# Two small PSUM tiles share the outcome's bank, and the routing work changes its steps: linear attention and mixture of experts on one core

## The chip, the cores and the metric

The kernel runs on one core of a Trainium2 chip. The metric is the device time of the whole program in microseconds (us). Five engines work from their own instruction queues and wait for one another by semaphores: TensorE (PE) multiplies matrices and writes to PSUM; VectorE (DVE) and ScalarE (ACT) read PSUM and SBUF; GpSimd (POOL) reads SBUF and issues the indirect DMAs; SyncE (SP) issues the plain DMAs. All data is fp32.

## The reference, cut to what matters

x has 4 batches of 2048 tokens with 256 features. Two sublayers are added to it, each scaled by rows that come from a small conditioning vector (`sa, ca, ga, sb, cb, gb`).

```python
h = _layernorm(x) * (1 + ca) + sa
q, k, v = (phi(h @ Wq), phi(h @ Wk), h @ Wv)     # phi = elu + 1, 16 heads of 16
S = S + k_t[:, None] * v_t[None, :]; z = z + k_t # running over the tokens
num = S . q_t ; den = max(z . q_t, 1e-6)
x = x + ga * ((num / den) @ w_out.T)
h = _layernorm(x) * (1 + cb) + sb
logits = h @ w_router.T                          # 8 experts, the two best per token
keep = position_in_expert < capacity             # a running count over the tokens, 1280 each
y = sum_e combine[:, e] * (silu(h @ w_gate.T) @ w_down[e].T)
x = x + gb * y
```

## The kernel before

The 8192 tokens are cut into 16 **groups** of 512 (`G`), each of 4 tiles of 128. The main loop runs over s = 0 to 64, `g, j = divmod(s, 4)`: one **step** j per tile. The order of the instructions of PE, ACT, DVE and POOL is the order of the program text (`manual_schedule`), so the loop's body is a hand-written pipeline over several groups. While the attention of group g runs, the keys, queries, values and denominators of `nxt` = g+1 are made, group `nrm` = g+2 is normalised and its keys projected, group `far` = g+3 gets its sums, group `prv` = g-1 is normalised for the second sublayer and its router logits and ranks are found, and group `old` = g-2 gets its positions and slots and is sent off, row by row, to a list per expert in DRAM. Group 14 takes a branch of its own (`early`), and group 15 is the `tail`. After the loop comes the expert phase: the lists are read back in blocks, multiplied with the gate and down matrices, and added to the output by indirect DMAs.

What each step does, with the names that matter below:

- At its head every step has the scores of its tile (L494, into the four banks of `psc`), masked by VectorE (L500) to `at`; `attend` (L570) for the tile of the step before; `keep_state` (L514); and `take_out`, in which ScalarE copies the outcome and the state's gain from the bank `po` to `both` (L525) and POOL adds the state up (`s_acc` L538, `s_msk` L540). `from_state` (L557) ends the step with the first products for the next `po`. `done()` is the output projection of the tile before (`pw` L588), its addition to x (L589) and its statistics (L325); each step calls it once.
- Step 0: two query projections (`pq` L375), `second_moments` and `deviations` (mean and spread for both norms; ScalarE's squares L309, POOL's L295, L296, L313, L315, L317), first half of `running_keys` (a scan on VectorE, L433, and POOL's product with q, L438).
- Step 1: `keys_by_token`, `positions(old)`, second half of `running_keys`, `values` (L397, copied by L405), `normalise` of `nrm`, `shift_rows(old)` (adds the row `sb`, L618).
- Step 2: `denominators` (`pd` L446, then `den` L451 and `rden` L453 on VectorE), `second_norm(prv)`, `to_features` of `nrm` (`pta`), `scaled_q` (`pr` L464 from `rden`, written to the banks of `psc`; L471 reads it), `dispatch(old)` (the slots: fourteen small VectorE instructions, L731 to L753), `to_features` of `prv` (`ptm`).
- Step 3: `logits(prv)` (`pl` L640, copied to `lgT`), `scale_rows(prv)` (POOL L612), `send(old, 0, 3)`, `heads_apart` (`qeo` L484), the first k projection of `nrm`, `logits_by_token` (`lt` L653), `ranks` (L669 to L699: VectorE finds maximum and difference, ScalarE the exponential L672, VectorE the rest, POOL the counts), `done()`, the second k projection, `finish_keys` (L389), `sums(far)` (ScalarE L282).

PSUM has 8 banks. `psc` takes four, `po` one, and every other product takes one of three that go round (`bank()`). A tile in such a bank keeps it until its last reader is done:

```python
ps = ctx.enter_context(tc.tile_pool(name="ps", bufs=3, space=PSUM))
...
ps_sc = tokens.enter_context(tc.tile_pool(name="ps_sc", bufs=1, space=PSUM))
ps_o = tokens.enter_context(tc.tile_pool(name="ps_o", bufs=1, space=PSUM))
...
def bank(name):
    return ps.tile([P, 512], F32, tag="bank", name=name)
```

Of the kernel before, what the change touches and what calls it, by code (L numbers as in the profile page):

```python
# [36 lines left out]
F32 = mybir.dt.float32  # L37
AF = mybir.ActivationFunctionType
ALU = mybir.AluOpType
AX = mybir.AxisListType  # L40

P = 128
# [14 lines left out]
GATE_EPS = 1e-6  # L57
I32 = mybir.dt.int32
SLOTS = NE * CAP
O_GB, O_CW, O_TOK, W = D, 2 * D, 2 * D + NE, 2 * D + NE + 4  # L60
FAR = 65536.0
HB = 3
# [5 lines left out]
def adaln_block(ctx: ExitStack, tc, x, wqkvT, woutT, wrT, wgT, wdT, cT, wmod, out):  # L68
# [8 lines left out]
    def bank(name):  # L77
        return ps.tile([P, 512], F32, tag="bank", name=name)
# [207 lines left out]
    def second_moments(g):  # L286
# [8 lines left out]
        nc.gpsimd.tensor_scalar(ve[:, :NT], mv[:, :, 1], LN_EPS, None, ALU.add)  # L295
        nc.gpsimd.tensor_scalar(nm[:, :NT], mv[:, :, 0], -1.0, None, ALU.mult)  # L296

    def deviations(m, a):

        nm = G_.pop("nm")  # L300
        ve = G_.pop("ve", None)
        lo, hi = 0 if m is not None else NT, 2 * NT if a is not None else NT
        if ve is None:
            ve = small.tile([P, 2 * NT], F32, tag="ve", name=f"vea_{a}")
        if a is not None:
            xn = G_["xna", a]
            sq = small.tile([P, NT], F32, tag="sqa", name=f"sqa_{a}")
            for j in range(NT):
                nc.scalar.activation(  # L309
                    xn[:, j, :], xs[a][:, j, :], AF.Square, bias=nm[:, NT + j : NT + j + 1],  # L310
                    accum_out=sq[:, j : j + 1],
                )
            nc.gpsimd.tensor_scalar(ve[:, NT:], sq, 1.0 / D, LN_EPS, ALU.mult, ALU.add)  # L313
        rstd = small.tile([P, 2 * NT], F32, tag="rstd", name=f"rstd_{m}_{a}")
        nc.gpsimd.tensor_tensor(rstd[:, lo:hi], ve[:, lo:hi], mhalf[:, lo:hi], ALU.pow)  # L315
        nmr = small.tile([P, 2 * NT], F32, tag="nmr", name=f"nmr_{m}_{a}")
        nc.gpsimd.tensor_tensor(nmr[:, lo:hi], nm[:, lo:hi], rstd[:, lo:hi], ALU.mult)  # L317
        G_["ns", "m"] = nmr[:, :NT], rstd[:, :NT]
        G_["ns", "a"] = nmr[:, NT:], rstd[:, NT:]
# [117 lines left out]
            )  # L437
            nc.gpsimd.tensor_tensor(G_["qs", g][:, h, :], zc[:, h, :], G_["q", g][:, h, :], ALU.mult)  # L438

    def denominators(g):  # L440

        zq = G_["qs", g]
        pd = bank(f"pd_{g}")
        for h in range(NH):
            for j in range(NT):
                nc.tensor.matmul(  # L446
                    pd[32 * j : 32 * j + 32, :P], hpick[:, h, :], zq[:, h, j * P : (j + 1) * P],
                    start=(h == 0), stop=(h == NH - 1),
                )
        den = small.tile([P, P], F32, tag="den", name=f"den_{g}")  # L450
        nc.vector.tensor_scalar(den, pd[:, :P], DEN_EPS, None, ALU.max)  # L451
        rden = small.tile([P, P], F32, tag="rden", name=f"rden_{g}")
        inst = nc.vector.reciprocal(rden, den)  # L453
        G_["rden", g] = rden
        return inst
# [191 lines left out]

    state = {}

    def logits_by_token(part):  # L650
        g, j0, n = part
        lt = G_["lt", part] = bank(f"lt_{g}_{j0}")
        nc.tensor.transpose(lt[:, : 32 * n], G_.pop(("lgT", part))[: 32 * n, :], ident[: 32 * n, : 32 * n])  # L653

    def ranks(part, count=nc.gpsimd):
        g, j0, n = part
        if ("lt", part) not in G_:
            logits_by_token(part)
        lt = G_.pop(("lt", part))
        lg = lt[:, : 32 * n].rearrange("p (j e) -> p j e", j=n)[:, :, :NE]  # L660

        def tile_(name, shape, **kw):
            return small.tile([P, NT] + shape, F32, tag=name, name=f"{name}_{g}_{j0}", **kw)[:, :n]

        def wide(t):
            return t.unsqueeze(2).to_broadcast([P, n, NE])

        mx = tile_("mx", [])
        nc.vector.tensor_reduce(mx, lg, AX.X, ALU.max)  # L669
        gt_ = tile_("gates", [NE])  # L670
        nc.vector.tensor_tensor(gt_, lg, wide(mx), ALU.subtract)  # L671
        nc.scalar.activation(gt_, gt_, AF.Exp)  # L672
        sm = tile_("sm", [])
        nc.vector.tensor_reduce(sm, gt_, AX.X, ALU.add)
        nc.vector.reciprocal(sm, sm)
        nc.vector.tensor_tensor(gt_, gt_, wide(sm), ALU.mult)

        shape = [P, n, NE, NE]
        other = gt_.unsqueeze(2).to_broadcast(shape)
        own = gt_.unsqueeze(3).to_broadcast(shape)  # L680
        ahead = tile_("ahead", [NE, NE], bufs=1)
        nc.vector.tensor_tensor(ahead, other, own, ALU.is_gt)
        tie = tile_("tie", [NE, NE], bufs=1)
        nc.vector.tensor_tensor(tie, other, own, ALU.is_equal)
        nc.vector.tensor_tensor(tie, tie, tri8.unsqueeze(1).to_broadcast(shape), ALU.mult)
        nc.vector.tensor_tensor(ahead, ahead, tie, ALU.add)
        mask = tile_("mask", [NE])
        rank = tile_("rank", [NE])
        nc.vector.tensor_reduce(rank, ahead, AX.X, ALU.add)
        nc.vector.tensor_scalar(mask, rank, 1.5, None, ALU.is_lt)  # L690


        cnt = small.tile([P, NT + 1, NE], F32, tag="cnt", name=f"cnt_{g}_{j0}")
        if "cnt" not in state:
            count.memset(cnt[:, 0, :], 0.0)
        else:
            count.tensor_copy(cnt[:, 0, :], state["cnt"])
        for j in range(n):
            count.tensor_tensor(cnt[:, j + 1, :], cnt[:, j, :], mask[:, j, :], ALU.add)  # L699
        state["cnt"] = cnt[:, n, :]  # L700
        G_["route", part] = gt_, mask, rank, cnt
# [157 lines left out]
    with tc.manual_schedule(engines={ET.PE, ET.Activation, ET.DVE, ET.Pool}):  # L859
# [40 lines left out]
        for s in range(NG * NT + 1):  # L900
# [21 lines left out]
                logits(prv)  # L922
            if prv is not None and j == 3 and not early:
                scale_rows(prv)
            if last is not None:
                attend(*last)
            grow = g < NG and not (g % GPB == GPB - 1 and j == NT - 1)
# [4 lines left out]
            if tail:  # L932
# [27 lines left out]
                else:  # L960
# [15 lines left out]
                    positions(p15b)  # L976
                    dispatch(p15b)
                    send(p15b, 0, 4)
            if old is not None and j == 3 and not early:
                send(old, 0, 3)  # L980
            if s == 0:
                free_slots(2, project(1, "k", 0, D, 2))
                free_slots(3, project(1, "k", 1, D, 2))
# [8 lines left out]
            elif j == 0:  # L992
# [8 lines left out]
                    deviations(g - 1 if prv is not None else None, nrm)  # L1001
                if nxt is not None:
                    running_keys(nxt, (0,))
            elif j == 1:
                if nxt is not None:
                    keys_by_token(nxt)
# [5 lines left out]
                if nxt is not None:  # L1012
                    running_keys(nxt, (1,))
                if g >= 3:
                    send((g - 3, 0, NT), 3, 6)
                if nxt is not None:
                    values(nxt, 0)
                    values(nxt, 2)
                if nrm is not None:
                    normalise((nrm, 0, NT), "a", xs[nrm], G_["xna", nrm])  # L1020
                if old is not None:
                    shift_rows(old)
                if early:
                    to_features(prv, "m", 2)
                    dispatch(old)
                if g + 4 < NG:
                    load_x(g + 4)
            elif j == 2:
                if g >= 3:
                    send((g - 3, 0, NT), 6, 8)  # L1030
                if nxt is not None:
                    denominators(nxt)
                if early:
                    logits_by_token(prv)
                    scale_rows(prv)
                    send(old, 0, 4)
                elif prv is not None:
                    second_norm(prv)
                if nrm is not None:
                    to_features((nrm, 0, NT), "a", 0)  # L1040
                done()
                if nxt is not None:
                    scaled_q(nxt)
                if early:
                    ranks(prv)
                elif old is not None:
                    dispatch(old)
                if prv is not None and not early:
                    to_features(prv, "m", 2)
            else:  # L1050
                if nxt is not None:
                    heads_apart(nxt, (0,))
                if nrm is not None:
                    project(nrm, "k", 0, D, 2, later=True)
                if nxt is not None:
                    heads_apart(nxt, (1,))
                if prv is not None and not early:
                    logits_by_token(prv)
                    ranks(prv)
                done()  # L1060
                if early:
                    send(old, 4, 8)
                    positions(prv)
                    dispatch(prv)
                    shift_rows(prv)
                if nrm is not None:
                    project(nrm, "k", 1, D, 2, later=True)
                if nrm is not None:
                    finish_keys(nrm)
                if g % GPB == GPB - 1 and g + 1 < NG:  # L1070
                    gated_out(g // GPB + 1)
                if far is not None:
                    sums(far)
            last = None
            if g < NG:
                from_state(g, j)
# [64 lines left out]
```

## Time and profile before

| | |
|---|---|
| time, median of 3 runs | 910.64 us (909.93 to 918.53) |
| the profiled execution: time, span of its instructions | 915.75 us, 913.8 us |
| mean granted TensorE clock | 0.96 |
| busy: PE, DVE, POOL, ACT | 823.0, 568.2, 477.1, 419.0 us |
| main loop (scores of group 0 to the last sends) | about 62 to 600 us |
| expert phase | about 604 to 914 us |

In the profile, a row of a timeline gives the start, the duration, the engine, the line of the kernel, the operation, the tile written and the tiles read, and in brackets how long the engine had been idle and what ended that. A group of instructions is given as one row with count, busy time, mean, and idle time before it. "PEld" is the loading of weights on TensorE, which runs beside its multiplications. PEclk is the share of the full clock that TensorE was granted.

### The profile page before, as it was taken

The numbers are of one execution on the slowest core, as the hardware profiler recorded it, in microseconds if no ns is written. First come the engines' busy times: TensorE is split into PE (matmuls) and PEld (weight loads), VectorE is DVE, ScalarE is ACT, GpSimd is POOL, SyncE is SP. The second block draws the span as 40 slices with busy tenths as digits, with TensorE's granted clock in tenths as the row PEclk, the third lists the DMA queues.
The fourth block names the chain that finished last, engine by engine and source line by source line (L and its number), as shares of the span: only waits on it lengthen the run. The fifth ranks groups of instructions, "written<-read, shape, count | busy, mean of one in ns | idle before, by whom it ended". The sixth has DMA issues, their size and how long they took to land.

```text
span 913.8 us, 20612 instructions
## 1 busy us (share of the span) xinstructions
PE 823.0 (90%) x8245; PEld 576.5 (63%) x8245; DVE 568.2 (62%) x1158; ACT 419.0 (46%) x972; POOL 477.1 (52%) x605
## 2 busy tenths in 40 slices
PE   6899979999999899999999976539999999999995
PEld 4477657567567567567667555326776767767764
DVE  3667768988888888888988886513333333333331
ACT  4557656656567567566566423212222222222220
POOL 2323446575586586576676586523443444434434
PEclk9999989999999999999999989659999999999998
DMA  8499851331442242432121111255665656545233
GB/s 307 135 358 347 188 110 72 124 136 66 129 136 68 105 136 69 120 111 77 61 76 55 49 49 39 66 200 134 148 138 106 134 112 145 110 100 112 35 34 41
DMA packets 75111, 108.25 MB, mean 118 GB/s; under 512 B 9578, under 2 KB 47218, under 8 KB 75016
## 3 DMA queue, kind: packets, MB, share of 16 engines
q1 hardware_dynamic: 47672, 68.91, 24.8%
q0 software_dynamic: 21760, 31.99, 16.3%
q10 hardware_dynamic: 5584, 6.04, 2.0%
q8 instruction: 65, 1.06, 0.5%
q14 instruction: 30, 0.25, 0.1%
HBM read 45.07 MB, written 74.69 MB: 131 GB/s over the span
## 4 chain that ended last, share of the span: by engine, by line
PE 66%; DVE 15%; issue 6%; POOL 5%; ACT 4%; DMA 2%; POOLq 0%; DVEq 0%; ACTq 0%; SPq 0%
PE ph L821 14%; PE pe L834 13%; PE pq L375 6%; PE pv L397 5%; PE psc L494 5%; PE pk L375 5%; PE po L570 5%; PE pw L588 4%; DVE at L500 3%; PE po L557 3%; DVE sel L751 2%; DVE qs L471 2%; POOL slots L770 2%; PE pte L810 2%; POOL out_dram L843 1%
## 5 line engine op out<-in xcount | busy, mean ns | idle before, releaser
L843 POOL DMA_INDIRECT out_dram<-y,tok x80 | 123.3, 1542 | 180.7 <-DVE y L839 126.2
L500 DVE TENSOR_TENSOR at<-psc,tri 128x1024 f32<-128x1024 f32 x128 | 150.1, 1214 | 29.2 <-PE psc L494 28.8
L770 POOL DMA_INDIRECT slots<-hrow,idx x128 | 129.4, 1011 | 52.5 <-issue 36.4
L821 PE MATMUL ph<-hTe,wg_sb 128*128 128x512 f32 (+1 forms) x384 | 153.5, 527 | 0.0
L834 PE MATMUL pe<-wd,hid 128*128 128x256 f32 x640 | 150.5, 379 | 0.0
L827 DVE SCALAR_TENSOR_TENSOR hid<-th,ph 128x512 f32<-128x512 f32 (+1 forms) x96 | 57.5, 599 | 146.3 <-ACT th L826 146.3
L834 PEld LDWEIGHTS pe<-wd,hid 128*128 128x128 f32 x640 | 121.6, 190 | 37.0 <-issue 23.0
L826 ACT ACTIVATE th<-ph 128x512 f32<-128x512 f32 (+1 forms) x96 | 50.5, 526 | 156.4 <-PE ph L821 156.4
L821 PEld LDWEIGHTS ph<-hTe,wg_sb 128*128 128x128 f32 x384 | 70.4, 193 | 39.0 <-issue 32.5
L375 PE MATMUL pk<-hTa,wqkv_sb 128*128 128x512 f32 x128 | 69.3, 671 | 22.6 <-DVE gates L671 22.6
L494 PE MATMUL psc<-qeo,k 32*128 32x256 f32 x1024 | 74.7, 405 | 2.4 <-DVE qs L471 1.0
L588 PE MATMUL pw<-wob,both 128*128 128x256 f32 x236 | 63.2, 391 | 7.8 <-ACT both L525 5.5
L570 PE MATMUL po<-at,vpad 128*32 128x128 f32 x2048 | 69.8, 278 | 0.0
L839 DVE SCALAR_TENSOR_TENSOR y<-pe,rows 128x256 f32<-128x256 f32 x80 | 38.7, 484 | 49.6 <-PE pe L834 49.6
L570 PEld LDWEIGHTS po<-at,vpad 128*32 128x32 f32 x2048 | 53.9, 111 | 17.1 <-issue 16.9
L375 PE MATMUL pq<-hTa,wqkv_sb 128*128 128x512 f32 x128 | 61.3, 604 | 0.0
L494 PEld LDWEIGHTS psc<-qeo,k 32*128 32x128 f32 x1024 | 47.8, 188 | 19.7 <-issue 13.3
L397 PE MATMUL pv<-wqkv_sb,hTa 128*128 128x256 f32 x256 | 59.2, 384 | 0.0
L588 PEld LDWEIGHTS pw<-wob,both 128*128 128x128 f32 x236 | 41.9, 192 | 25.1 <-issue 10.1
L813 ACT COPY hTe<-pte 128x512 f32<-128x512 f32 (+1 forms) x48 | 24.7, 514 | 70.8 <-PE pte L810 70.6
L375 PEld LDWEIGHTS pk<-hTa,wqkv_sb 128*128 128x128 f32 x128 | 23.5, 201 | 46.7 <-issue 44.9
L397 PEld LDWEIGHTS pv<-wqkv_sb,hTa 128*128 128x128 f32 x256 | 47.6, 190 | 6.5 <-issue 0.4
(166 smaller groups left out, 1348.3 us busy)
## 6 DMA issues: line engine op xcount, KB each, us to landing
slots<-free SPq DMA_DIRECT2D x80, 262.0 KB, 5.1
rows<-slots SPq DMA_DIRECT2D x16, 1048.0 KB, 6.1
x<-in_x_dram SPq DMA_DIRECT2D x16, 512.0 KB, 6.1
out_dram<-x SPq DMA_DIRECT2D x16, 512.0 KB, 2.9
hrow<-mod_d SPq DMA_DIRECT2D x48, 128.0 KB, 3.5
rows<-slots SPq DMA_DIRECT2D x8, 524.0 KB, 7.6
wd<-in_wdT_dram ACTq DMA_DIRECT2D x8, 512.0 KB, 4.6
slots<-hrow,idx POOLq DMA_INDIRECT x128, 2.9
```

The costliest lines, as they stand in the source:

```text
L375: nc.tensor.matmul(pq, wqkv_sb[:, k, o + h * P : o + (h + 1) * P], hT[:, k, :], start=(k == 0), stop=(k == NH - 1))
L397: nc.tensor.matmul(pv[:, i * D : (i + 1) * D], hT[:, k, (j + i) * P : (j + i + 1) * P], wqkv_sb[:, k, 2 * D : 3 * D], start=(k == 0), stop ...
L494: nc.tensor.matmul(psc[:, a, h], kT[r : r + 32, h, cols], qeo[r : r + 32, h, :, cols], start=True, stop=True,)
L500: masked = nc.vector.tensor_tensor(at, psc[:, 2 * m : 2 * m + 2].rearrange("p i h q t -> p (i h q) t"), tri.unsqueeze(1).to_broadcast([P, ...
L570: nc.tensor.matmul(po[32 * a : 32 * a + 32, h * P : (h + 1) * P], vp[:, j, h * 4 + a, q : q + 2, :], att[a // 2][:, a % 2, h, q, :], start ...
L588: nc.tensor.matmul(pw[:, :D], oT[:, h, :], wob[:, h, :], start=(h == 0), stop=(h == NH - 1))
L770: row = nc.gpsimd.indirect_dma_start(out=slots[:, :], out_offset=bass.IndirectOffsetOnAxis(ap=idx[:, c, j : j + 1], axis=0), in_=hr[:, j0 ...
L821: nc.tensor.matmul(ph[:, :m], wg_sb[:, k, f * P : (f + 1) * P], hTs[b][:, k, :m], start=(k == 0), stop=(k == NH - 1),)
L826: nc.scalar.activation(th[:, :m], ph[:, :m], AF.Tanh, scale=0.5)
L827: nc.vector.scalar_tensor_tensor(hids[b][:, f, :m], th[:, :m], 1.0, ph[:, :m], ALU.add, ALU.mult)
L834: nc.tensor.matmul(pe[:, :D], hids[b][:, f, j * P : (j + 1) * P], wds[e][:, f, :], start=(f == 0), stop=(f == NF - 1),)
L843: put = nc.gpsimd.indirect_dma_start(out=out[:, :], out_offset=bass.IndirectOffsetOnAxis(ap=toks[b][:, j : j + 1], axis=0), in_=y, in_offs ...
```

## The change

Two small tiles leave the three banks that go round: `pd` (the denominators, 128 columns) and `lt` (the logits by token, 128 columns) are put into columns 320 to 447 of the bank of `po`, whose columns 0 to 319 hold the outcome and the state's gain. `denominators` follows `to_features` of `nrm` instead of leading it. `done()` is called in the middle of `ranks`, ahead of the exponential. ScalarE's passes that use no bank go to the heads of steps, ahead of `take_out`: `squares` (out of `deviations`) in step 0, `second_norm` in step 2, `sums` in step 3. `normalise` of `nrm` goes ahead of `values`. `shift_rows` moves from step 1 to step 0, `dispatch` from step 2 to step 1, and the eight sends of a group now lie in steps 2 (three), 3 (three) and the next step 1 (two).

```diff
+O_SMALL = D + NH * 32
...
+    def squares(a):
+
+        xn, nm = G_["xna", a], G_["nm"]
+        sq = G_["sq", a] = small.tile([P, NT], F32, tag="sqa", name=f"sqa_{a}")
+        for j in range(NT):
+            nc.scalar.activation(
+                xn[:, j, :], xs[a][:, j, :], AF.Square, bias=nm[:, NT + j : NT + j + 1],
+                accum_out=sq[:, j : j + 1],
+            )
+
     def deviations(m, a):
 
+        if a is not None and ("sq", a) not in G_:
+            squares(a)
...
-            for j in range(NT):
-                nc.scalar.activation(
-                    xn[:, j, :], xs[a][:, j, :], AF.Square, bias=nm[:, NT + j : NT + j + 1],
-                    accum_out=sq[:, j : j + 1],
-                )
...
-    def denominators(g):
+    def denominators(g, beside=False):
...
-        pd = bank(f"pd_{g}")
+        pd = G_["po"][:, O_SMALL : O_SMALL + P] if beside else bank(f"pd_{g}")[:, :P]
...
-    def logits_by_token(part):
+    def logits_by_token(part, beside=False):
         g, j0, n = part
-        lt = G_["lt", part] = bank(f"lt_{g}_{j0}")
+        lt = G_["po"][:, O_SMALL : O_SMALL + P] if beside else bank(f"lt_{g}_{j0}")
+        G_["lt", part] = lt
...
-    def ranks(part, count=nc.gpsimd):
+    def ranks(part, count=nc.gpsimd, meanwhile=None):
...
+        if meanwhile is not None:
+            meanwhile()
         nc.scalar.activation(gt_, gt_, AF.Exp)
...
                 scale_rows(prv)
+            if prv is not None and j == 2 and not early:
+                second_norm(prv)
+            if not tail and j == 0 and s > 0 and nrm is not None:
+                squares(nrm)
+            if not tail and j == 3 and far is not None:
+                sums(far)
             if last is not None:
                 attend(*last)
...
-            if old is not None and j == 3 and not early:
-                send(old, 0, 3)
+            if old is not None and j in (2, 3) and not early:
+                send(old, 3 * (j - 2), 3 * (j - 1))
...
                     running_keys(nxt, (0,))
+                if old is not None:
+                    shift_rows(old)
             elif j == 1:
...
                 if g >= 3:
-                    send((g - 3, 0, NT), 3, 6)
+                    send((g - 3, 0, NT), 6, 8)
+                if nrm is not None:
+                    normalise((nrm, 0, NT), "a", xs[nrm], G_["xna", nrm])
                 if nxt is not None:
                     values(nxt, 0)
                     values(nxt, 2)
-                if nrm is not None:
-                    normalise((nrm, 0, NT), "a", xs[nrm], G_["xna", nrm])
-                if old is not None:
-                    shift_rows(old)
                 if early:
                     to_features(prv, "m", 2)
+                if old is not None:
                     dispatch(old)
...
             elif j == 2:
-                if g >= 3:
-                    send((g - 3, 0, NT), 6, 8)
-                if nxt is not None:
-                    denominators(nxt)
                 if early:
...
-                elif prv is not None:
-                    second_norm(prv)
                 if nrm is not None:
                     to_features((nrm, 0, NT), "a", 0)
+                if nxt is not None:
+                    denominators(nxt, beside=True)
                 done()
                 if nxt is not None:
                     scaled_q(nxt)
                 if early:
                     ranks(prv)
-                elif old is not None:
-                    dispatch(old)
...
                 if prv is not None and not early:
-                    logits_by_token(prv)
-                    ranks(prv)
-                done()
+                    logits_by_token(prv, beside=True)
+                    ranks(prv, meanwhile=done)
+                else:
+                    done()
...
-                if far is not None:
-                    sums(far)
```

More of the change, by code (lines that the diff above doesn't have):

```diff
@@ L305, in deviations @@
         if a is not None:
-            xn = G_["xna", a]
-            sq = small.tile([P, NT], F32, tag="sqa", name=f"sqa_{a}")
-            for j in range(NT):
-                nc.scalar.activation(
-                    xn[:, j, :], xs[a][:, j, :], AF.Square, bias=nm[:, NT + j : NT + j + 1],
-                    accum_out=sq[:, j : j + 1],
-                )
-            nc.gpsimd.tensor_scalar(ve[:, NT:], sq, 1.0 / D, LN_EPS, ALU.mult, ALU.add)
+            nc.gpsimd.tensor_scalar(ve[:, NT:], G_.pop(("sq", a)), 1.0 / D, LN_EPS, ALU.mult, ALU.add)
         rstd = small.tile([P, 2 * NT], F32, tag="rstd", name=f"rstd_{m}_{a}")
@@ L446, in denominators @@
                 nc.tensor.matmul(
-                    pd[32 * j : 32 * j + 32, :P], hpick[:, h, :], zq[:, h, j * P : (j + 1) * P],
+                    pd[32 * j : 32 * j + 32, :], hpick[:, h, :], zq[:, h, j * P : (j + 1) * P],
                     start=(h == 0), stop=(h == NH - 1),
@@ L450, in denominators @@
         den = small.tile([P, P], F32, tag="den", name=f"den_{g}")
-        nc.vector.tensor_scalar(den, pd[:, :P], DEN_EPS, None, ALU.max)
+        nc.vector.tensor_scalar(den, pd, DEN_EPS, None, ALU.max)
         rden = small.tile([P, P], F32, tag="rden", name=f"rden_{g}")
```

## Prediction

> **What bounds the kernel now.** I read the page's engine sums first, then its costliest groups for a TensorE line with idle time, then the timeline engine by engine.
>
> ```profile
> PE 823.0 (90%) x8245; PEld 576.5 (63%) x8245; DVE 568.2 (62%) x1158; ACT 419.0 (46%) x972; POOL 477.1 (52%) x605
> L375 PE MATMUL pk<-hTa,wqkv_sb 128*128 128x512 f32 x128 | 69.3, 671 | 22.6 <-DVE gates L671 22.6
> ```
>
> PE is 90% busy, and its largest idle item that one line owns is 22.6 us before the key projection, ended by VectorE's L671. Asked for the readers of `lt`, the trace gives twelve such waits: one in the fourth step (j = 3) of each of groups 2 to 13. The timeline of PE in group 8, with the same place in group 7:
>
> ```profile
> 305.04 3.38 PE L375 MATMUL pk<-hTa,wqkv_sb 128*128 128x512 f32 x4 [2.20 <-DVE gates L671]
> ...
> 332.19 1.15 PE L494 MATMUL psc<-qeo,k 32*128 32x256 f32 x16
> ...
> 336.66 0.27 PE L653 MATMUL lt<-ident,lgT 128*128 128x128 f32 x1
> 336.77 1.03 PE L588 MATMUL pw<-wob,both 128*128 128x256 f32 x4
> 339.73 1.95 PE L375 MATMUL pk<-hTa,wqkv_sb 128*128 128x512 f32 x4 [1.93 <-DVE gates L671]
> ```
>
> The second k projection wants one of three banks, and `lt` sits in it until VectorE has read it. VectorE is late, as its timeline (and POOL's, last row) shows:
>
> ```profile
> 334.34 2.02 DVE L751 SCALAR_TENSOR_TENSOR sel<-rank,slot 128x32 f32<-128x32 f32 x1
> ...
> 336.92 2.34 DVE L500 TENSOR_TENSOR at<-psc,tri 128x1024 f32<-128x1024 f32 x2
> ...
> 339.39 0.19 DVE L671 TENSOR_TENSOR gates<-lt,mx 128x32 f32<-128x32 f32 x1
> ...
> 339.88 0.19 DVE L674 TENSOR_REDUCE sm<-gates 128x4 f32<-128x32 f32 x1 [0.29 <-ACT gates L672]
> ...
> 344.80 2.34 DVE L500 TENSOR_TENSOR at<-psc,tri 128x1024 f32<-128x1024 f32 x2
> ...
> 359.24 2.36 DVE L500 TENSOR_TENSOR at<-psc,tri 128x1024 f32<-128x1024 f32 x2 [1.38 <-PE psc L494]
> ...
> 361.83 0.95 DVE L453 RECIPROCAL rden<-den 128x128 f32<-128x128 f32 x1
> ```
>
> ```profile
> 333.94 2.37 POOL L612 TENSOR_TENSOR hrow<-hrow,modr 128x1024 f32<-128x1024 f32 x1
> ```
>
> The last instructions of `dispatch` run into step 3, and one `sel` takes 2.02 us instead of 0.18: it ends 0.05 us after POOL's L612. From scores to scores of step 3 (332.19 to 365.29) a loop over a group is 33.1 us. Loops in which the stall is followed by a slow clock are 34.6; group 7's shows in the windows view, PEclk being the third number from the right:
>
> ```profile
> 302.01:305.43 3.42, 1.22 (x5) 0.68 (x4) 2.93 (x7) 2.42 (x5) 2.23 (x3) 1.00 0.20 78
> 305.43:308.84 3.41, 3.41 (x16) 1.14 (x18) 3.17 (x10) 0.39 (x1) 1.62 (x4) 0.50 0.45 173
> ```
>
> Five of the twelve stalls end like this. The slow stretches are 3.41 us and start on one grid of 3.41 us; laying the idle stretches on that grid, each with 1.86 us or more inside one cell got one, none with 1.80 or less did. The mean loop from the step-3 mask of group 2 (133.61) to that of group 13 (503.77) is 370.16/11 = 33.65 us.
>
> **The change, part by part.**
>
> *Banks.* `lt` moves into the outcome's bank, so the wait for L671 goes. Without it step 3 to step 0 on PE is 7.82 us (group 1, which has no such wait: 92.50 to 100.32) instead of 9.99. `pd` moves too; its matmuls must follow ScalarE's copy out of that bank, and to_features(a), now ahead of them, covers that. PE's own work is unchanged: 7.82 + 7.28 + 8.56 + 7.1 = 30.75 us a loop. That is PE's floor. What is late next is VectorE.
>
> *Sums at the head of step 3.* ScalarE's four sums (0.40 each, 1.6 together) now stand ahead of the copy `both`, qeo, ex/k, qeo and the Exp of `ranks`. Counted from the scores of step 3: lgT at 1.79 as in group 9, +0.2, sums 1.6, `both` 0.33, qeo pair 1.24, ex and k 1.0, qeo pair 1.24, so the Exp runs from 7.4 to 7.6. In group 1, which waits for nothing, it ran from 6.86. The values `lt` are there at 4.8, gates done at 5.2, x and stats (now between) done at 6.5: VectorE then waits for the Exp until 7.65. Before, its `sm` began at 7.69. So being early at `lt` buys the rank chain nothing. From `sm` to mask 2.92; then finish_keys 1.21, with x and stats (0.8) already done: the next step-0 mask multiplication starts at 11.8 instead of 12.6.
>
> *Shift in step 0, dispatch in step 1.* Before, VectorE went from that multiplication (344.80) to the one of step 2 (359.24) in 14.44 us, with shift inside and 2.6 of waiting for PE and ScalarE. After, in order: mask 2.26, q 0.61, x 0.45, stats 0.34, aggregates 0.36, q 0.61, scan 1.2, shift 1.2 = 7.03; mask 2.24, x and stats 0.79, scan 1.2, dispatch 3.0 = 7.23; no wait is left in it. Group 14 already runs dispatch in step 1 (its `early` branch):
>
> ```profile
> 524.71 2.16 POOL L438 TENSOR_TENSOR qs<-zc,q 128x512 f32<-128x512 f32 x1 [1.93 <-DVE zc L433]
> ```
>
> ```profile
> 525.65 1.25 DVE L731 TENSOR_SCALAR slot<-pos 128x32 f32<-128x32 f32 x1
> ```
>
> ```profile
> 533.24 0.73 PE L464 MATMUL pr<-rden,spread 32*128 32x128 f32 x16 [1.48 <-DVE rden L453]
> ```
>
> POOL's product of the second scan comes due as dispatch begins and holds VectorE for 1.1 us. It is the same pair here: +1.2. The first product can catch the second scan as it does now (1.71 for 1.28): +0.2. The blocked `sel` (1.84) goes, since L612 now runs beside L471 and the masks, which it does not slow. So 7.03 + 7.23 + 1.4 = 15.7 us instead of 14.44.
>
> *The sum.* VectorE's loop: 33.1 - 0.8 (mask of step 0 earlier) + 1.25 (15.7 for 14.44) - 0.2 (`pr` no longer waits for `pw`) = 33.3 us. PE's floor is 30.75, so PE now stands about 2.5 us before `pr`, waiting for `rden`, where it stood 2.1 before `pk`: the stall moves from step 3 to step 2.
>
> *The clock.* A stall of 2.4 to 2.5 us puts 1.86 or more into one cell of the grid in (3.41 - 2.45 + 2 x 0.6)/3.41 = 0.63 of positions, against 0.42 seen now. A slow stretch costs 1.55 now (34.6 less 33.1); after `pr` it slows pr, ptm, scores and logits, 3.8 us of work all on the loop: I take 1.3. Mean loop 33.3 + 0.63 x 1.3 = 34.1. The Trainium skill ("TensorE: Matmul & The Clock Gate", HAM oscillation) has it that idle gaps up to about 3.4 us leave the clock alone; by that the loop would be 33.3, and the time 915.75 - 12 x 0.35 = 911.5. The trace shows that 1.86 is enough, so I take the row: 915.75 + 12 x 0.45 = 921.
>
> *The rest, at nothing.* Squares at the head of step 0 and second_norm at that of step 2 (2.0 us each) delay `both` to about 3.2 and 18.8 us after the step-0 scores, ahead of `pw` at 4.0 and 19.5. Normalise ahead of the value copies ends near 15.1, so the copies end near 16.4, before PE wants their banks at 18. If that cover went, PE would wait in a place where it now has 2.5 us to give. POOL: sends two in step 1, three in 2, three in 3 (1.3 each, eight as now), the token numbers 0.25 ahead of s_acc, all where s_msk has a step of slack. SP: the rows' mod_d loads stay in step 2 behind load_x, and their buffer is sent a step sooner. L295, L296, L313 meet q, scan and shift, and each ends with them, as L296 does in group 1 (1.07 for 0.23); they do not hold VectorE.
>
> *Unknown: L315.* The pow takes 1.67 us on POOL and in every group of before lies beside a mask, which it leaves alone; no row has it beside a two-input VectorE instruction. Low end 0; high end 1.65 a loop, if it starts in the gap ahead of shift, for which the Trainium skill ("SBUF — State Buffer", Who interferes with whom) speaks: the shared port pair is held for the whole instruction. I take 0: the small POOL products ahead of it are each held by q, scan, shift, which pushes it beside the mask of step 1.
>
> **Against the median.** The profiled execution took 915.75, 5.1 above the median: about three slow stretches more, at 1.55 each, since stalls of 1.8 to 1.9 lie on the edge. After the change they lie over it. From the median: 910.64 - 2 x 1.55 + 12 x 0.2 + 12 x 0.63 x 1.3 = 920. I forecast **920**.
>
> **Rivals.** (1) *PE becomes the bound*: dispatch's blocked time and the Exp's delay do not meet on VectorE, whose plain work is 27.4 us a loop (33.1 less 3.4 idle and 2.3 held by POOL). Then 30.75: 915.75 - 12 x 2.9 = 881. For it: VectorE has room. Against it: the 4.5 us (33.3 less 1.4 less 27.4) that it must wait in step 3 (scores, `lt`, `pw`, Exp). With the Exp's wait kept but dispatch unblocked, 32.1 and no slow stretch: 897. (2) *The two halves cancel*: the stall lands near 1.9, the clock as often slow as now: 911. (3) *L315 catches shift*: loop 33.3 + 1.65, PE idle 4 us, nearly every loop with a slow stretch (1.2): 36.1, so 915.75 + 12 x 2.5 = 945.
>
> **Numbers.** The stall that moves, with its slow stretches (own range 910 to 930): 0.5, two fifths of it within 1%. Rival 1 with its half form: 0.2. Rival 2: 0.1. Rival 3 and other new waits: 0.2. So faster by over 1% 0.2, within 1% (about what a measurement can tell from no change) 0.3, slower by over 1% 0.5. The range goes from 893, just under the half form, to 940, short of rival 3.
>
> **What would show it.** Right: no wait for L671 at L375; `pr` L464 waiting some 2.5 us for `rden` in groups 2 to 13; `sm` idle over 1 us for the Exp; L732 or a neighbour at 1.2 us beside L438; slow stretches after step 2. Wrong: `pr` without a wait, or loops near 31 us; or L315 beside shift with shift over 2 us.

## The result, and the profile after

The changed kernel takes 919.37 us (median of 14 runs, 917.38 to 923.0); the kernel before, run beside it, takes 912.87 (909.25 to 920.47). The ratio is 1.0052, interval 1.0029 to 1.0075: 0.5% slower, with 1 outside the interval, but too little to count as a change. The profiled execution took 921.98 us (span 920.3), where that of before took 915.75. The lines have moved by six to nine: L381 is the projection (was L375), L470 `pr` (L464), L444 POOL's product with q (L438), L748 an instruction of `dispatch` (L739).

The page's engine sums and its group of k projections, after:

```profile
PE 829.5 (90%) x8245; PEld 585.6 (64%) x8245; DVE 551.4 (60%) x1158; ACT 414.2 (45%) x972; POOL 486.1 (53%) x605
L381 PE MATMUL pk<-hTa,wqkv_sb 128*128 128x512 f32 x128 | 63.6, 623 | 0.0
```

The last number of the second row was 22.6: the wait for the logits is gone completely. The engine sums say nothing of it, and PE is still 90% busy. The list of waits of PE between 200 and 500 us (total, times, longest) and PE's timeline tell where the stall is now:

```profile
PE pr L470 <- DVE rden L459: 17.6, 8, 2.6
```

```profile
335.38 0.86 PE L470 MATMUL pr<-rden,spread 32*128 32x128 f32 x16 [2.62 <-DVE rden L459]
...
339.08 1.21 PE L500 MATMUL psc<-qeo,k 32*128 32x256 f32 x16
...
346.96 1.15 PE L500 MATMUL psc<-qeo,k 32*128 32x256 f32 x16
...
369.82 1.13 PE L470 MATMUL pr<-rden,spread 32*128 32x128 f32 x16 [2.07 <-DVE rden L459]
370.88 1.97 PE L367 MATMUL ptm<-ident,hrow 128*128 128x128 f32 x8
```

Each of groups 3 to 13 has one stall ahead of `pr`, in step 2, of 2.0 to 2.6 us (1.58 in group 3), where the loop had one of about 1.9 ahead of `pk`, in step 3. Step 3 to step 0 is now 346.96 - 339.08 = 7.88 us. The last row is slow: the eight transposes take 1.97 us, against 1.09 at the full clock. VectorE's timeline of the same loop, with two rows of POOL's:

```profile
346.68 0.18 DVE L683 TENSOR_REDUCE sm<-gates 128x4 f32<-128x32 f32 x1 [1.01 <-ACT gates L681]
...
350.82 2.34 DVE L506 TENSOR_TENSOR at<-psc,tri 128x1024 f32<-128x1024 f32 x2
...
357.81 2.35 DVE L506 TENSOR_TENSOR at<-psc,tri 128x1024 f32<-128x1024 f32 x2
...
360.87 1.45 DVE L439 TENSOR_TENSOR_SCAN zc<-ones_g,zc,k 128x512 f32<-128x512 f32 x1
...
363.06 1.15 DVE L748 TENSOR_TENSOR gates<-gates,keep 128x32 f32<-128x32 f32 x1
...
366.14 2.35 DVE L506 TENSOR_TENSOR at<-psc,tri 128x1024 f32<-128x1024 f32 x2
...
368.72 0.95 DVE L459 RECIPROCAL rden<-den 128x128 f32<-128x128 f32 x1
```

```profile
358.04 1.67 POOL L321 TENSOR_TENSOR rstd<-ve,mhalf 128x8 f32<-128x8 f32 x1
...
362.84 1.33 POOL L444 TENSOR_TENSOR qs<-zc,q 128x512 f32<-128x512 f32 x1
```

From the step-0 mask (350.82) to `rden` VectorE stands once, for 0.21 us: it is the chain. L748 takes 1.15 us where it takes 0.19 in a loop in which nothing holds it (399.09), and ends 0.04 us after POOL's L444 does. The pow of L321 lies wholly beside the mask of step 1.

**Where the 6.5 us between the two spans lie.** The ten loops between the step-3 scores of groups 2 and 12 take 343.1 us instead of 336.7, so +6.4: 34.31 a loop for 33.67. The loops at both ends of this stretch give back 4.4. Most of that is the loop from group 13 to group 14, 33.07 instead of 36.54, which before had both stalls, the one for the logits in step 3 and the one for `rden` that group 14's own branch already showed. The start costs 4.7 (step-3 scores of group 1 at 97.2, not 92.5), and what follows group 14 nothing (-0.1). Of the 4.7, 3.2 lie ahead of the first scores, with which the main loop begins (39.7 us here, 36.5 before, 36.3 and 36.5 in two of the experiments below). About 3 of them are the clock: it rises to its full value at 18.4 us, not 15.3, which costs the first k projections 1.4 us, and it is slow again from 35.5 to 38.9 us, which costs L222 1.5. The two experiments have neither.

### The profile page after: what moved, and what is told of

Same layout as the page of the kernel before. It is cut to its first block, busy times and chain, and to the rows that moved or that the text cites. A ratio compares the mean times of both kernels' runs of the same rounds, so it can differ in the third digit from the quotient of the medians.

```text
span 920.3 us, 20625 instructions
## 1 busy us (share of the span) xinstructions
PE 829.5 (90%) x8245; PEld 585.6 (64%) x8245; DVE 551.4 (60%) x1158; ACT 414.2 (45%) x972; POOL 486.1 (53%) x605
## 4 chain that ended last, share of the span: by engine, by line
PE 67%; DVE 17%; issue 6%; POOL 3%; DMA 3%; ACT 2%; SPq 1%; POOLq 0%; DVEq 0%; ACTq 0%
PE ph L830 14%; PE pe L843 13%; PE pk L381 7%; PE pq L381 6%; PE psc L500 5%; DVE at L506 5%; PE po L576 4%; PE pw L594 4%; DVE zc L439 3%; PE po L563 2%; PE ptm L367 2%; PE pv L403 2%; PE pte L819 2%; DVE rden L459 1%; POOL out_dram L852 1%
## 5 line engine op out<-in xcount | busy, mean ns | idle before, releaser
L381 PE MATMUL pk<-hTa,wqkv_sb 128*128 128x512 f32 x128 | 63.6, 623 | 0.0
L381 PE MATMUL pq<-hTa,wqkv_sb 128*128 128x512 f32 x128 | 61.3, 604 | 0.0
L368 ACT ACTIVATE hTm<-ptm,modc 128x512 f32<-128x512 f32 (+1 forms) x34 | 24.7, 751 | 62.5 <-PE ptm L367 61.9
```

The costliest lines, as they stand in the source:

```text
L381: nc.tensor.matmul(pq, wqkv_sb[:, k, o + h * P : o + (h + 1) * P], hT[:, k, :], start=(k == 0), stop=(k == NH - 1))
```

## The experiments

The ratios are to the kernel before, on the same chip.

### First chip: one part at a time (kernel before: 913.86 us)

**The logits alone.** The kernel before, with only this:

```diff
-        lt = G_["lt", part] = bank(f"lt_{g}_{j0}")
+        lt = G_["po"][:, O_SMALL : O_SMALL + P] if beside else bank(f"lt_{g}_{j0}")
...
-                    logits_by_token(prv)
+                    logits_by_token(prv, beside=True)
```

> The kernel before with one edit: the logits by token lie in the outcome's bank; order of the work, dispatch in step 2, sums and squares as before. Theory (VectorE's loop bounds the changed kernel because shift and dispatch stand ahead of the mask of step 2 and the sums ahead of the Exp): here VectorE's loop is 12.6 to the mask of step 0, 11.8 of work to the mask of step 2, 3.5 to rden and 2.35 to the next scores, 30.2 us, so PE's floor of 30.75 bounds, with some 0.3 us more in step 3, where from_state must wait for the read of lt: loop 31.0 us, no slow stretches, no wait over 1 us at pr; time near 885. Rival (VectorE simply has too much work, whatever its order): the stall only moves to another place, loop 33 us, time 908 to 920.

Measured: 885.56 us, ratio 0.9697 (0.9654 to 0.974). The eleven loops from group 2 to 13 take 30.8 to 31.3 us, nine of them under 31, and between 129 and 504 us the clock is never lowered. PE's longest waits from 130 to 500 us, all of them together 3 us:

```profile
PE pw L589 <- DVE den L452: 1.4, 8, 0.2
PE psc L495 <- DVE at L501: 0.6, 3, 0.2
```

One hand-over of a bank is worth 3%, and PE stands at its floor (30.75 in the prediction's sum). The rest of the change takes all of this back. VectorE is nearly as late for the logits as it was (6.9 us after the scores of step 3, not 7.2), but now nobody waits for it.

**ScalarE's order undone.** The changed kernel with `sums` back at the end of step 3 and `squares` back in `deviations`:

```diff
-            if not tail and j == 0 and s > 0 and nrm is not None:
-                squares(nrm)
-            if not tail and j == 3 and far is not None:
-                sums(far)
...
+                if far is not None:
+                    sums(far)
```

> The changed kernel with ScalarE's sums back at the end of step 3 and the squares back in deviations; second_norm stays at the head of step 2. Theory: the Exp runs 0.5 to 0.6 us earlier, so the mask of step 0, rden and the loop are 0.6 us earlier: loop 32.2 without a slow stretch (32.85 in the changed kernel), the wait for rden 1.4 to 1.5 us, under what brings a slow stretch, so that most of those go too: time 895 to 903. Rival (the sums do not matter, dispatch alone does): 917 to 921.

Measured: 918.5 us, ratio 1.0069 (1.0044 to 1.0094): as the changed kernel. The Exp does come earlier, and VectorE's timeline (idle time in brackets) shows what takes its place:

```profile
339.95 0.19 DVE L683 TENSOR_REDUCE sm<-gates 128x4 f32<-128x32 f32 x1 [0.59 <-ACT gates L681]
...
348.58 0.69 DVE L390 SCALAR_TENSOR_TENSOR q<-exq,q 128x512 f32<-128x512 f32 x1 [0.48 <-ACT q L386]
```

`sm` waits 0.59 instead of 1.01, and then the second `q` waits 0.48, which it did not. Two chains end together at this `q`: scores, logits, Exp, ranks, mask on the one side, PE's query projection, ScalarE's exponential, q on the other. Shortening one is worth nothing. So the expectation failed, and with it the idea that the wait for the Exp is a cause of its own.

**Dispatch back in step 2.** The changed kernel with `dispatch` where it was (shown), and the sends too:

```diff
-                if old is not None:
-                    dispatch(old)
                 if g + 4 < NG:
                     load_x(g + 4)
...
                 if early:
                     ranks(prv)
+                elif old is not None:
+                    dispatch(old)
```

> The changed kernel with dispatch back in step 2, behind scaled_q, and the sends back where they were before (three in step 3, three in the next step 1, two in the next step 2); shift in step 0, banks, sums, squares as changed. Theory: VectorE's chain from the mask of step 0 to rden loses 4.0 us (dispatch 3.0, held 1.0), PE's floor bounds: loop 31.0, no wait for rden over 0.5 us, no slow stretches in the middle groups, time 879 to 886; the sel held by L612 (2.0 us) is back and costs nothing. Rival (the sums ahead of the Exp are the cost): 910 to 920.

Measured: 901.49 us, ratio 0.9871 (0.9828 to 0.9914). The placing of dispatch and the sends, which this does not part, is 1.8 points of the 3.55 that separate the changed kernel from the logits alone. It was expected to be nearly all. PE's waits from 130 to 500 us (total, times, longest) show what else this kernel has and the one with the logits alone has not, and a loop's timeline where it comes from:

```profile
PE po L563 <- DVE gates L678: 9.3, 10, 1.2
PE pr L470 <- DVE rden L459: 5.6, 11, 0.6
```

```profile
415.90 0.29 DVE L457 TENSOR_SCALAR den<-po 128x128 f32<-128x128 f32 x1 [0.45 <-PE po L452]
...
419.83 0.97 POOL L779 DMA_INDIRECT slots<-hrow,idx  x1 [0.30 <-issue]
...
419.88 0.19 DVE L742 TENSOR_TENSOR slot<-slot,eoff 128x32 f32<-128x32 f32 x1
...
420.21 3.05 DVE L748 TENSOR_TENSOR gates<-gates,keep 128x32 f32<-128x32 f32 x1
420.82 2.38 POOL L618 TENSOR_TENSOR hrow<-hrow,modr 128x1024 f32<-128x1024 f32 x1
...
428.01 0.64 PE L563 MATMUL po<-qs,s_msk 32*32 32x128 f32 x16 [1.14 <-DVE gates L678]
```

The denominators, now behind the transposes, come 0.45 us too late for `den`, and so `pr` waits 0.56. And `from_state` (L563), which wants to write the outcome's bank again, waits for VectorE's last reader of the logits in it: from group 3 on, one instruction of dispatch in every loop takes 2.7 to 3.1 us and ends with POOL's L618 (about 1.9 with the logits alone), so the ranks start late: VectorE reads the logits 8.0 us after the scores. The shared bank has a hand-over of its own. These waits, 1.4 us a loop together, are as long as the 1.3 by which the loop (32.2 in the median) is longer than with the logits alone. That they are its cause is argued from this agreement; taking them away one by one on this chip was not done.

**More work on PE.** The changed kernel with the 16 matmuls of the denominators done four times, which adds 1.3 us of work a loop ahead of `pr`:

```diff
-        for h in range(NH):
+        for h in [h for _ in range(4 if beside else 1) for h in range(NH)]:
```

> The changed kernel with the sixteen matmuls of the denominators done four times over, into the same place with the same values: 1.5 us of work more on TensorE in each step 2, in the time in which it waits for rden. Theory (the stall itself costs nothing more than VectorE's loop, and the slow clock that follows it costs 1.5 us in four of five loops): the idle stretch falls under 1 us, the slow stretches in groups 2 to 13 go, loop 32.85 us, time 900 to 904, faster by 17 us with more work. Rival (the slow clock is hidden beside VectorE): no change, 919. Rival (PE is the bound): slower, 937.

Measured: 908.16 us, ratio 0.9956 (0.993 to 0.9981), so about 1% less than the changed kernel with more to do. All loops of groups 2 to 13 take 32.7 to 33.0 us, and no slow stretch falls between 38.8 and 547 us. The stall is still there, shorter, in PE's waits from 130 to 500 us:

```profile
PE pr L470 <- DVE rden L459: 10.0, 12, 1.3
```

VectorE's chain is unchanged, and so is the loop without a slow clock, 32.9; what went is the clock. It was expected some 4 to 8 us lower. Part of that is the extra work itself: in groups 0 and 1 nothing stalls that would take it up, and the step-3 scores of group 1 come at 99.8 us, 2.6 later than in the changed kernel.

### Second and third chip

On two other chips the kernel before takes 963.62 and 962.22 us; ratios hold within one chip only. The changed kernel itself was not run on them.

The four kernels on the second chip were: the logits alone plus the placing of `shift_rows`, `dispatch` and the sends as changed; the changed kernel with the logits back in the banks that go round (`beside=True` taken away in step 3); the logits alone plus the denominators in the outcome's bank behind `to_features`; and the changed kernel with `dispatch` ahead of the second scan:

```diff
+                if old is not None:
+                    dispatch(old)
                 if nxt is not None:
                     running_keys(nxt, (1,))
...
-                if old is not None:
-                    dispatch(old)
                 if g + 4 < NG:
```

> The kernel with the logits by token beside (885.6) and, of the rest of the change, only what moves the routing: shift_rows in step 0, dispatch in step 1, the sends as changed. ScalarE's passes, normalise and the denominators stay as before. Theory (the place of dispatch ahead of the mask of step 2 is what takes the gain back): rden comes late again, loop 33.0 to 33.2 us without a slow stretch, a wait of 2 us at pr, slow stretches in most loops, time 916 to 922. Rival (ScalarE's passes at the heads, or the shared bank of pd, take it back): 885 to 890.

> The changed kernel with the logits by token back in one of the three banks that go round; all else as changed. Theory (in the changed kernel VectorE is early at lt, having read it 5.2 us after the scores of step 3 where PE needs the bank at 5.4, so the bank is no longer short): no wait for the read of lt at the second k projection, time as the changed kernel, 917 to 922. Rival (the shared bank still does part of the work): a wait there again, 925 to 940.

> The kernel with the logits by token beside (885.6) with the denominators moved too: pd into the outcome's bank and behind to_features of nrm. Theory: where VectorE is not late, pd comes 1.0 us later, den waits for it about 0.4 us (0.45 in the kernel with dispatch back), rden and pr with it: loop 31.3 for 30.95, no slow stretches, 888 to 892. Rival (pd's place costs nothing): 885.

> The changed kernel with one call moved within step 1: dispatch stands ahead of the second scan instead of behind it, so that POOL's second product L444 meets the mask of step 2, which it does not hold, instead of dispatch. Theory (VectorE from q to rden is the loop, 1.0 us of it the hold): rden 0.8 us earlier, loop 32.0 to 32.1, the idle stretch before pr about 1.2 us and under what brings a slow stretch, time 890 to 896. Rival (the hold is hidden, or another product holds VectorE for as long): 917 to 921.

Measured, in this order: 921.94 (ratio 0.9562, 0.9527 to 0.9598), 923.73 (0.9593, 0.9557 to 0.9629), 947.74 (0.9831, 0.9792 to 0.987) and 928.18 (0.9637, 0.9599 to 0.9676). The third and fourth are far from what was expected. The first two numbers look like it, but the first not for the reason given: its loops are 33.6 to 33.75 (two are longer) with no slow stretch and no wait for `rden`. The second says little by its time, since the changed kernel was not run beside it, but its trace shows what was expected: VectorE reads the logits 4.9 to 5.0 us after the scores of step 3 (once 6.9), and from 130 to 500 us the k projection never waits for that read, though the logits lie in one of the three banks. On this chip at least, the new order of the changed kernel takes that wait away without the shared bank. The first, third and fourth were run again with the logits alone beside them:

> The kernel before with only the logits by token in the outcome's bank (beside=True), once more, as the anchor of this call. If TensorE's instructions come without pauses, as in the first call: 0.97 of the kernel before, loops of 30.9 us. If a loop again has a pause of 2.3 to 4 us in TensorE's own instruction supply (rows marked issue, as in the second call, where the kernel before took 963 us): the floor of 30.9 rises by the pause, loops of 33.5 to 35 us, and the gain over the kernel before stays, since the kernel before has both the pause and its wait.

> The kernel with lt alone moved, plus the change's placing of shift (step 0), dispatch (step 1) and the sends. Theory (VectorE's chain from the step-0 mask to rden sets the loop once dispatch stands in step 1): scores of step 0 to the row product pr take 23.05 us as in this kernel's earlier trace, plus 7.7 and 2.4, so 33.2 us a loop with 2.3 us of TensorE waiting for rden, slow stretches after it, 34.2 to 34.5 with them: 911 to 924 us where the kernel with lt alone takes 885, a ratio to that one of 1.03 to 1.045. Rival (the placing alone costs nothing; the loss needs the denominators' move or ScalarE's new order): within 1% of the kernel with lt alone. With TensorE paused by itself as in the second call, the pause lies where it would wait anyway: about 33.7 a loop, and the two kernels stand close together.

> The kernel with lt alone moved, plus the denominators in the outcome's bank behind to_features. Theory: VectorE is early at den here (dispatch comes after it), so the later pd costs only what TensorE's order moves, under 0.4 us a loop: within 1% of the kernel with lt alone, 885 to 892 us. Rival (the move of pd is what costs): pd must follow ScalarE's copy of the outcome, den and rden come 1 us or more later and pr waits: 897 us or more, a ratio to lt alone of 1.015 or more. With TensorE paused by itself ahead of that copy, as in the second call, the rival's wait is on the path and adds to the pause: 1.02 to 1.03 of the kernel before less.

> The changed kernel with dispatch ahead of the second scan in step 1, so that POOL's product of that scan no longer stands beside dispatch. Theory (dispatch held by that product is 1.0 of VectorE's chain): scores of step 0 to pr 22.3 us as in this kernel's earlier trace, plus 7.8 and 2.3, so 32.4 a loop, TensorE idle about 1.5 ahead of pr, under the 1.8 that brings a slow stretch; 34.3 less 32.4 over twelve loops, 919 to 896 (893 to 900), a ratio to the kernel before of 0.98. Rival (the hold is made up elsewhere, by the pow beside shift, which was 2.58 us there): loops of 33 with slow stretches, 910 to 920.

Measured on the third chip: logits alone 936.06 (0.9745, 0.9673 to 0.9818), with the placing of dispatch 919.58 (0.9571, 0.9498 to 0.9645), with the denominators moved 945.02 (0.9838, 0.9764 to 0.9911), the changed kernel with dispatch first 924.69 (0.9621, 0.9549 to 0.9694). PE's timeline shows why these don't rank as on the first chip; the kernel with logits and dispatch, then the one with dispatch first:

```profile
323.69 0.61 PE L447 MATMUL pd<-qs,hpick 128*32 128x128 f32 x7
324.64 0.41 PE L447 MATMUL pd<-qs,hpick 128*32 128x128 f32 x4 [0.34 <-issue]
325.36 0.32 PE L447 MATMUL pd<-qs,hpick 128*32 128x128 f32 x2 [0.31 <-issue]
326.07 0.41 PE L447 MATMUL pd<-qs,hpick 128*32 128x128 f32 x3 [0.40 <-issue]
```

```profile
335.55 0.53 PE L576 MATMUL po<-at,vpad 128*32 128x128 f32 x9
336.39 0.44 PE L576 MATMUL po<-at,vpad 128*32 128x128 f32 x5 [0.30 <-issue]
337.13 0.45 PE L576 MATMUL po<-at,vpad 128*32 128x128 f32 x5 [0.31 <-issue]
```

The sixteen matmuls of the denominators take 2.8 us, where on the first chip they take 0.62. "Issue" means that the trace shows nothing they wait for; these traces hold about a tenth fewer semaphore records than those of the first chip, so that a wait may be hidden. Nearly every loop loses 2 to 4 us like this, at one place for each kernel, beside POOL's sends. In the kernel with the logits alone little of it is marked issue: in one loop ScalarE's copy `both` starts 3.2 us after PE's L515 has ended (0.3 on the first chip), and PE then waits 1.7. There the loss is added to the floor, and with four slow stretches the loops are 34.0 to 35.6. In the kernel with logits and dispatch the pause lies ahead of `pr`, where the changed kernel waits 2.0 to 2.6 us for VectorE on the first chip; that it is free there is argued from this, and its loop is 33.6. In the one with the denominators moved, ScalarE's copy is held with it and the denominators with the copy:

```profile
PE po L447 <- ACT both L526: 21.7, 8, 2.9
```

(PE's waits from 130 to 500 us, third chip.) What was expected for paused chips holds for the logits alone; for the denominators the wait is as expected, but costs 1.0% and not 1.5 or more; for the placing the loop is as expected, but the time is 1.8% below the logits alone and not close to it. For dispatch first, neither theory nor rival held: loops of 34.1 us, of which about 2 are the pause, at a place where PE had nothing to spare. Only its loop from group 2 to 3 has no pause: 31.72 us with L748 at 0.19, where the same loop of the changed kernel on the first chip takes 32.80 with L748 at 1.15. That is one loop, but it is the size and the direction that were expected of the hold. What each of these three would do on a chip without pauses is otherwise open. So is the cause of the pause. The expectations lay it to TensorE's own instruction supply, which no run shows: in the kernel with logits and dispatch, PE pauses between 257 and 260 us, and no transfer of instructions starts from 252.2 to 260.

## Why the prediction was right, and where it was not

The forecast was 920 us, by a stall that moves from step 3 to step 2. The stall did so, and the time is 919.37. That the two agree to 1 us is in part luck: the forecast added 9.4 us to a kernel before of 910.64, and measured are 6.5 on one of 912.87. The greatest chance, 0.5, stood on slower by over 1%; what came is 0.5% slower, in the class that had 0.3.

- **Banks.** Right. No wait for the logits is left, and step 3 to step 0 is 7.88 us (predicted 7.82). That the move alone is worth 3% follows from the first experiment; the prediction's floor of 30.75 was met at 30.93. But in the changed kernel the new order takes the same wait away by itself, as the logits put back in the three banks show (second chip).
- **Sums ahead of the Exp.** The times are right: the Exp starts 346.42 - 339.08 = 7.34 us after the scores (predicted 7.4), `sm` at 7.60 (7.65), the step-0 mask at 11.74 (11.8). What does not follow is that this order costs anything: the second experiment shows q's chain ending with it.
- **Dispatch in step 1.** Right in kind: L748 takes 1.15 us beside POOL's product in eleven of twelve loops, the second scan takes 1.45. The chain from mask to mask is 366.14 - 350.82 = 15.32 us (predicted 15.7, before 14.44). Of the loss against the logits alone, the placing with the sends is half, by the third experiment; with it gone, two waits of the shared bank come out, for which the prediction has no term: `den` for the later denominators, and `from_state` for VectorE's read of the logits. In the changed kernel neither shows: VectorE comes to `den` late, and it reads the logits early (5.07 us after the scores in the loop shown, against 8.0), since dispatch no longer runs into step 3.
- **The loop.** Without a slow stretch it is 32.9 (32.8 and 32.94 in two loops; a third, of 33.76, begins just behind one), 0.4 less than the 33.3 of the sum, which is what the chain from mask to mask is shorter.
- **The clock.** The row was right against the rule. The Trainium skill ("TensorE: Matmul & The Clock Gate", HAM oscillation) lets gaps below about 3.4 us pass; here eight of the ten loops between groups 2 and 12 have a slow stretch behind a stall of 2.0 to 2.6 us, and with the stall filled to 1.3 at most the slow stretches are gone and 1% of the time with them (fourth experiment). The prediction's bound, 1.86 us inside one cell of the grid, also holds: all eight have 2.0 or more in one cell, and the two stalls without have 1.58, and 2.16 that lies as 1.18 and 0.98 in two cells. The sizes were off: the eight loops take 34.57 on average, so a slow stretch costs 1.7 us instead of 1.3, and it comes in 0.8 of the loops, not 0.63. With the shorter loop this gives a mean of 34.3, near the 34.1 of the sum, for two errors that in part cancel.
- **The sum.** It put 0.45 us on each of twelve loops. Measured are 0.64 on each of ten, -4.4 for the loops at the ends and +4.7 for the start. The step that failed is the factor of twelve: the loop into group 14 had both stalls before, and one of them went. That the total agrees to 1 us (6.2 for 5.3) is partly luck, because the start's 3 us of slower clock are not the change's.
- **The pow on POOL.** Right: 1.67 us beside the mask of step 1. In two of twelve loops it lay beside shift, the prediction's unknown. One of them:

```profile
150.83 1.20 DVE L624 TENSOR_TENSOR hrow<-hrow,modr 128x1024 f32<-128x1024 f32 x1
150.99 2.58 POOL L321 TENSOR_TENSOR rstd<-ve,mhalf 128x8 f32<-128x8 f32 x1
```

Shift (L624) takes 1.20 us as in every other loop; it is the pow that takes longer (2.58 and 2.52).
- **Rivals.** PE never became the bound: the hold of L748 and the wait of `sm` both stand on VectorE. The half form (897) was not met even by the third experiment, which takes dispatch out of the chain. What `normalise` ahead of the values, `done()` inside `ranks` and second_norm at the head of step 2 are worth was not tried apart.

## What to carry to other kernels

When a wait is removed together with other moves, run the removal alone first: here it was worth 3%, and what was done beside it cost a little more than that. An edit that shortens one of two chains which end at the same instruction is worth nothing until the other is shortened too. Taking work out of the chain that bounds the loop counts, as with dispatch back in step 2; moving work into it lengthens it by the work and by what the instruction meets there, so look at what the neighbouring engine does at the new place.

## What was not expected of the hardware

- The slow clock can keep step with the loop. In the changed kernel its stretches start at 233.4, 267.6, 301.7, 335.8 and 370.0 us, 34.1 apart, and in the kernel with ScalarE's order undone at 226.7, 260.8, 294.9 and 329.1. Ten cells of the grid of 3.41 us are 34.1 us, and a loop with a slow stretch is 34.3 to 34.8, so the stall comes back at nearly the same place of the grid. It is no lock: `pr` starts at 232.15, 266.62, 301.04, 335.38 and 369.82 us, 34.3 to 34.5 apart, so the stall moves on by 0.2 to 0.3 us a loop, and after five it lies across two cells and is not followed by a slow stretch. The windows view shows one such cell and the next (PEclk third from the right):

```profile
335.60:339.00 3.40, 3.40 (x40) 2.50 (x36) 1.66 (x3) 1.55 (x2) 2.32 (x3) 0.54 0.76 252
339.00:342.40 3.40, 3.40 (x86) 2.67 (x83) 2.03 (x2) 1.47 (x8) 1.58 (x1) 0.96 0.44 168
```

- More work made the kernel faster: 1.3 us of matmuls a loop that add nothing to the result took 1% off.
- On two of the chips used, nearly every loop loses 2 to 4 us around PE without a wait that the trace explains, and the kernel before is 5% slower. On the first chip one loop of the third experiment has such a gap, of 2.89 us. The result of this document holds for the first chip: on the others, the changed kernel with one edit taken back or moved is about 4% faster than before, not 0.5% slower. Versions that are within a few per cent of each other have to be compared on more than one chip.
- A VectorE instruction of 32 columns took 3.05 us (third experiment). It began 0.6 us before POOL's product of 1024 columns did, while POOL issued an indirect send, and ended 0.05 after the product. The issue alone does not hold VectorE: L742, with two inputs too, takes its usual 0.19 us beside the same send, as do many others. Why the hold begins ahead of the product's record stays open.
